# A gated cross-attention and feed-forward layer on one core: input loads, weight stores, a PSUM bank and the helpers of the first group rearranged

## The chip, the core and the metric

The kernel runs on one core of one Trainium2 chip. The metric is the device time in microseconds (us) of one execution. Before the change the median of three runs is 2418.64 us (2414.57 to 2418.65). The profile is that of one more execution on the same core.

The core has a matrix engine (TensorE, PE in the profile, with its weight loads shown as PEld), three engines for element-wise work (VectorE or DVE, ScalarE or ACT, GpSimd or POOL), and SyncE (SP), which in this kernel only starts DMAs. A DMA can be started from several engines; each engine starts its own in the order of its instructions, so a start that has to wait holds up the starts, and any work, behind it on the same engine. SBUF is the on-chip memory that the engines work from, PSUM the eight banks that TensorE writes its sums to. "Scratch" below is a DRAM area that the kernel writes first and reads later.

## What is computed

All numbers are fp32: B = 64 sequences, S = 128, DIM = 512, four heads of 128, INTER = 1408.

```python
def attention(x, k, v, Wh, wg_w, wo_w, gamma, beta):   # k = v = ctx
    Q, K, V = (einsum('bshd,hde->bshe', heads(t), Wh) for t in (x, k, v))
    scores = einsum('bshe,bthe->bhst', Q, K) / sqrt(hd)
    masked = scores * decay[None]
    A = maximum(abs(masked.sum(axis=0)), 1.0)          # summed over all 64 sequences
    O = einsum('hst,bthe->bshe', A, V).reshape(b, s, dim)
    Y = (O - mean) / sqrt(var + 1e-3) * gamma + beta
    return relu(x @ wg_w) * Y @ wo_w
def ffn(x):
    g, u = (x @ gate_w.T) * gate_s, (x @ up_w.T) * up_s
    return (silu(g) * u) @ down_w.T * down_s
x = x + tanh(g_xattn) * attention(layernorm(x), ctx, ctx, ...)
return x + tanh(g_ffn) * ffn(layernorm(x))
```

The sum over all sequences in `A` is why the kernel has two passes: no attention output can be formed before every score is in.

## The kernel before

**Groups.** The work goes by groups of four sequences (512 tokens), so there are 16 groups. Products of large matrices use Strassen and Winograd's scheme: a matrix is split in 2 x 2 blocks, sums of blocks are formed first, and seven products of half size take the place of eight. The sums of the weights are formed once in the first pass and kept (`wgc`, in SBUF) or written to scratch (`wo_scr`, `dn_scr`, `gu_scr`); the sums of the activations are formed for every group (`combine_a` L190, `combine_b` L184).

**First pass (L393 to L409).** For each group:
- `prepare` (L315): statistics of x by VectorE (L150), one rstd for the four sequences (VectorE L145, then a power on GpSimd L146), then for each sequence the normalised rows xn (VectorE L162), four transposes on TensorE (L157), and their copy to `xnT` (VectorE or ScalarE, L329 and L331).
- `scores` of the group before (L334): x by the Gram matrix of Wh (pq L338, copied by ScalarE to q), and then 16 matmuls (L348) that add context by q to `acc`. `acc` is the second half of the PSUM tile `banks_c` (L134, L313) and takes the sum over all groups.
- `project` of the group before (L358): relu(x @ wg) by seven products (L169) into bank_a, bank_f, bank_b and the *first* half of `banks_c`. VectorE adds m5 to two results (L379, L382), ScalarE copies or applies relu to the others, and two stores bring w to scratch `w_scr` (L388).

`interleave` mixes the steps of these three by given weights. The order on each engine is then decided by the scheduler of the framework, which also adds the waits: it knows a dependency by tile, so two instructions on different halves of `banks_c` can wait for each other.

**Loads and stores.** Loads of x (L96, five buffers), of the context (L102, five buffers), the weights, and all stores are started by SyncE, in one order; ScalarE starts only the constants of the beginning (L203 to L217, among them `wgc`). From group 2 on, one step of `prepare_weights` (L247) is taken at the end of each group's turn: first wo, then six steps of down weights, then five of gate/up weights. Each step loads raw blocks into one buffer (tag "prep", L256, L273, L296), has GpSimd form the sums (L290, L305), and starts the stores of these sums (L264, L289, L309) in the same step. The sums of `wgc` are formed at the very start (L230), on GpSimd too.

**Between the passes.** After the last scores, `attn` is made from `acc` (L412 to L415). Attention of group 0 and the projection of group 15 are interleaved (L534).

**Second pass.** `attention(g)` (L418) runs interleaved with `ffn(g-1)` (L570). Attention: pv (L428) and po (L438) per sequence, normalisation of po, transposes (L455), scale and shift by ScalarE (L460), the product with w by GpSimd (L465), the sums ys by GpSimd (L471), and seven products with wo into bx, bz and by (L478). m1, a copy of the first of them, is added to three quarters of x by GpSimd (L496) and the rest by VectorE (L489); then comes the second LayerNorm (L520 to L529), whose transposed result is `x1nT`. The sums of x1nT's blocks are GpSimd's (`combine_tokens`, L549). Ffn: five blocks j of seven products (L169), of which each begins with

```python
bank_c = next_c()                              # L593: the other half of banks_c
nc.scalar.copy(bank_c, bank_a)                 # L596
product(bank_f, w[GS1], t[:, 0], True)         # L597
```

then the hidden values (L583, L584) and their sums, the rest of gate and up (L631), seven products with the down weights (L648) and, at the very end of a group, two stores of 512 KB (L697).

Of the kernel before, what the change touches and what calls it, by code (L numbers as in the profile page):

```python
# [1 line left out]

# [25 lines left out]
def interleave(*weighted):  # L28

    runs = [[gen, steps, 0] for gen, steps in weighted if gen is not None]  # L30
    while runs:
        run = min(runs, key=lambda r: (r[2] + 1) / r[1])
        try:
            next(run[0])
            run[2] += 1
        except StopIteration:
            runs.remove(run)


@with_exitstack  # L40
def flamingo_gated_layer(
# [63 lines left out]
    x_next = load_x(0)  # L105
    c_next = [load_ctx(b) for b in range(GB)]
# [27 lines left out]
    banks_c = ps_bank.tile([P, 2, TOK], F32, name="banks_c")  # L134
    for seeded in (bank_b, banks_c[:, 0, :]):
        for i in range(TOK // P):
            nc.tensor.matmul(
                seeded[:, i * P : (i + 1) * P], lhsT=ident, rhs=ident,
                start=(i == 0), stop=True, skip_group_check=True,
            )  # L140
# [58 lines left out]
    wide1 = pass1.enter_context(tc.tile_pool(name="wide1", bufs=2))  # L199
# [5 lines left out]
    for m, k, e in ((GA11, 0, 0), (GA12, 1, 0), (7, 0, 1), (GA22, 1, 1)):  # L205
        for s in range(2):
            e0 = e * HN + s * P
            nc.scalar.dma_start(
                out=wgc[:, m, s],
                in_=wg[k * HN : (k + 1) * HN, e0 : e0 + P].rearrange("(k p) i -> p k i", p=P),  # L210
            )
    decay = once.tile([P, H, S], F32, name="decay")
    nc.scalar.dma_start(out=decay, in_=decayT)
# [3 lines left out]
    nc.scalar.dma_start(out=wh_sb, in_=wh.rearrange("h d e -> d h e"))  # L217
# [6 lines left out]
    for h in range(H):  # L224
# [5 lines left out]
    combine_a(  # L230
        nc.gpsimd, [wgc[:, m] for m in (GS1, GS2, GS3, GS4)],
        wgc[:, GA11], wgc[:, GA12], wgc[:, 7], wgc[:, GA22],
    )

    def constants():

        nc.sync.dma_start(out=gamma_sb, in_=gamma.rearrange("(c p) -> p c", p=P))
        nc.sync.dma_start(out=beta_sb, in_=beta.rearrange("(c p) -> p c", p=P))
        nc.sync.dma_start(out=gs_sb, in_=gate_s)
        nc.sync.dma_start(out=us_sb, in_=up_s)  # L240
        cols = slice(REST * P, INTER)
        for s, w in enumerate((gateT, upT)):
            nc.sync.dma_start(
                out=gu_rest[:, s], in_=w[:, cols].rearrange("(c p) i -> p c i", p=P)
            )

    def prepare_weights():  # L247

        constants()
        ds = once.tile([P, DIM], F32, name="ds")  # L250
        nc.sync.dma_start(out=ds, in_=down_s.partition_broadcast(P))
        nc.vector.tensor_scalar_mul(ds, ds, tanh_g[:, 1:2])
        yield


        raw = once.tile([P, NC, DIM], F32, tag="prep", name="wo_raw")  # L256
        nc.sync.dma_start(out=raw, in_=wo.rearrange("(c p) e -> p c e", p=P))
        nc.vector.tensor_scalar_mul(raw, raw, tanh_g[:, 0:1])
        t = once.tile([P, 4, KC, HN], F32, tag="prep2", name="wo_t")
        b = (  # L260
            raw[:, 0:KC, 0:HN], raw[:, 0:KC, HN:DIM], raw[:, KC:NC, 0:HN], raw[:, KC:NC, HN:DIM],
        )
        combine_b(nc.gpsimd, [t[:, i] for i in range(4)], *b)
        for m, src in ((DB11, b[0]), (DB21, b[2]), (DB22, b[3])):  # L264
            nc.sync.dma_start(out=wo_scr[m], in_=src)
        for i, m in enumerate((DT1, DT2, DT3, DT4)):
            nc.sync.dma_start(out=wo_scr[m], in_=t[:, i])
        yield


        for j in range(NJ + 1):
            i1, i2 = (j, NJ + j) if j < NJ else (REST, None)
            raw = once.tile([P, 2, DIM], F32, tag="prep", name="dn_raw")  # L273
            for q, i in enumerate((i1, i2)):
                if i is None:
                    nc.sync.dma_start(out=raw[:, q], in_=downT[i1 * P : (i1 + 1) * P])
                    nc.gpsimd.tensor_tensor(dn_rest, raw[:, q], ds, ALU.mult)
                    continue
                if j == NJ:
                    continue  # L280
                nc.sync.dma_start(out=raw[:, q], in_=downT[i * P : (i + 1) * P])
                nc.gpsimd.tensor_tensor(raw[:, q], raw[:, q], ds, ALU.mult)
            if j == NJ:
                yield
                continue
            t = once.tile([P, 4, HN], F32, tag="prep2", name="dn_t")
            b = (raw[:, 0, 0:HN], raw[:, 0, HN:DIM], raw[:, 1, 0:HN], raw[:, 1, HN:DIM])
            combine_b(nc.gpsimd, [t[:, i] for i in range(4)], *b)
            for m, src in ((DB11, b[0]), (DB21, b[2]), (DB22, b[3])):  # L289
                nc.sync.dma_start(out=dn_scr[m, :, j], in_=src)  # L290
            for i, m in enumerate((DT1, DT2, DT3, DT4)):
                nc.sync.dma_start(out=dn_scr[m, :, j], in_=t[:, i])
            yield

        for j in range(NJ):
            w = once.tile([P, 8, 2, KC, P], F32, tag="prep", name="gu_raw")  # L296
            i1 = slice(j * P, (j + 1) * P)
            i2 = slice((NJ + j) * P, (NJ + j + 1) * P)
            k1, k2 = slice(0, HN), slice(HN, DIM)
            for s, mat in enumerate((gateT, upT)):  # L300
                for m, k, i in ((GA11, k1, i1), (7, k1, i2), (GA22, k2, i2), (GA12, k2, i1)):
                    nc.sync.dma_start(
                        out=w[:, m, s], in_=mat[k, i].rearrange("(c p) i -> p c i", p=P)
                    )
            combine_a(  # L305
                nc.gpsimd, [w[:, m] for m in (GS1, GS2, GS3, GS4)],
                w[:, GA11], w[:, GA12], w[:, 7], w[:, GA22],
            )
            nc.sync.dma_start(out=gu_scr[0][j], in_=w[:, 0:3])  # L309
            nc.sync.dma_start(out=gu_scr[1][j], in_=w[:, 3:7])  # L310
            yield

    acc = banks_c[:, 1, :].rearrange("p (h s) -> p h s", h=H)  # L313

    def prepare(g, x_t, xnT):  # L315

        for j in range(GB):
            bn(mean_var[:, g * GB + j, :], x_t[j // 2][:, j % 2, :])
        cols = slice(g * GB, (g + 1) * GB)
        inv_std(rstd[:, cols], mean_var[:, cols, 1], LN_EPS, GB)  # L320
# [37 lines left out]
    def project(g, xnT):  # L358
# [6 lines left out]
        bank_c = banks_c[:, 0, :]  # L365
# [21 lines left out]
        for q in range(2):  # L387
            nc.sync.dma_start(out=w_scr[g, q], in_=w[:, q])  # L388
# [4 lines left out]
    for g in range(NG):  # L393
        x_t, c_t = x_next, c_next
        xnT = wide1.tile([P, NC, TOK], F32, tag="xT", name="xnT")
        prep = prepare(g, x_t, xnT)
        next(prep)
        after = (g + 1) % NG
        x_next = load_x(after)
# [5 lines left out]
        c_next = [load_ctx(after * GB + j) for j in range(GB)]  # L405
        pending = (g, c_t, xnT)
        if g >= 2:
            next(weights, None)
# [9 lines left out]
    def attention(g, x_t, c_t, x1nT):  # L418

        yT = att.tile([P, NC, TOK], F32, tag="yT", name="yT")  # L420
        for q in range(2):
# [28 lines left out]
            for d in range(2):  # L450
# [14 lines left out]
                nc.gpsimd.tensor_tensor(y, w[:, d], y, ALU.mult)  # L465
# [5 lines left out]
        combine_a(nc.gpsimd, [s[:, i] for i in range(4)], a11, a12, a21, a22)  # L471
# [24 lines left out]
        for q, d in ((0, d2), (1, d1), (1, d2)):  # L496
            add(nc.gpsimd, q, d, m1)
# [34 lines left out]
    x_t, c_t = x_next, c_next  # L532
    x1nT = wide.tile([P, NC, TOK], F32, tag="xT", name="x1nT")
    interleave(  # L534
        (attention(0, x_t, c_t, x1nT), ATT_STEPS), (project(pending[0], pending[2]), 7)
# [9 lines left out]
    def next_c():  # L545
        turn[0] ^= 1
        return banks_c[:, turn[0], :]

    def combine_tokens(x1nT):  # L549

        t = comb.tile([P, 4, KC, HT], F32, tag="t", name="tcomb")
        b = as_b(x1nT)
        combine_b(nc.gpsimd, [t[:, i] for i in range(4)], *b)
        return b[0], b[2], b[3], t
# [15 lines left out]
    def ffn(g, x_t, x1nT, tokens):  # L570
# [87 lines left out]
        def down_rest(bank, q, cols):  # L658
            for i in range(2):
# [4 lines left out]
                    start=False, stop=(i == 1), skip_group_check=True,  # L664
# [27 lines left out]
        yield from down_product(bank_c, DT4, h22, False)  # L692
        down_rest(bank_c, 1, d1)
        add(1, d1, bank_c)
        for q in range(2):
            b = g * GB + 2 * q
            nc.sync.dma_start(out=out[b : b + 2].rearrange("b s d -> s b d"), in_=x_t[q])  # L697
# [3 lines left out]
    pending = (0, x_t, x1nT, combine_tokens(x1nT))  # L701
    x_next = load_x(1)
    c_next = [load_ctx(GB + j) for j in range(GB)]
    for g in range(1, NG):
        x_t, c_t = x_next, c_next
        x1nT = wide.tile([P, NC, TOK], F32, tag="xT", name="x1nT")
        if g + 1 < NG:
            x_next = load_x(g + 1)
# [6 lines left out]
        pending = (g, x_t, x1nT, combine_tokens(x1nT))  # L715
# [59 lines left out]
```

## Time and profile before

| | |
|---|---|
| median of three runs | 2418.64 us (2414.57 to 2418.65) |
| the profiled execution | 2416.87 us |
| its span, first to last instruction | 2415.1 us |
| mean granted clock of TensorE | 0.994 |
| TensorE busy: matmuls, weight loads | 2351.8 us (97%), 1996.3 us (83%) |
| VectorE, ScalarE, GpSimd busy | 802.0, 587.2 and 686.2 us (33%, 24%, 28%) |
| moved by DMA | 396.31 MB, mean 164 GB/s |
| load of x, 512 KB: from start to landing | 5.0 us (median of 64) |
| load of context, 256 KB | 3.0 us (median of 128) |
| store of w, 512 KB | 3.7 us (median of 32) |
| chain of work that ended last | TensorE 85%, VectorE 5%, GpSimd 4%, DMA 3% |

The page cuts the span into 40 slices of 60.4 us. In the rows of slices a digit is the busy share of an engine in tenths, and 9 means 90% or more; in the row PEclk it is the clock that was granted to TensorE, in tenths of full speed. The first pass with the join takes about the first seven slices (to 420 us), the second pass the rest, at 125.38 us a group.

Rows of instructions are read like this: the time of the start, the duration, the engine with the line of the code, the operation, its output and inputs by the program's names, and in brackets how long the engine had been idle just before and what ended that. A row of waits names the waiting instruction, then what it waited for, and behind it the total in us, the number of times and the longest. In a table by windows each engine has its busy time and, in brackets, the number of instructions, in the order PE, PEld, DVE, ACT, POOL; behind them stand the mean clock, the DMA engines' busy share and the GB/s that they moved. "SPq" marks a DMA that SyncE starts.

### The profile page before, as it was taken

Reading aid. Unit: us, or ns where it says so; the run is one execution under the profiler, and the core shown is the slowest. Engines: PE = TensorE matmul, PEld = TensorE weight load, DVE = VectorE, ACT = ScalarE, POOL = GpSimd, SP = SyncE. Lnnn points to the kernel's source line nnn. Section 1 sums busy time; section 2 is a strip of 40 time slices with the busy share of each in tenths; the row PEclk is TensorE's granted clock in tenths of the full one; section 3 lists DMA queues with packets and bytes.
Section 4 is the critical chain, followed back from the end, with each engine's and each line's share of the span. In section 5 each row is a group of like instructions: output and inputs, shape, how many; then the busy total and the mean of one; then the engine's idle time right before and its main releaser. Section 6 shows DMA issues by size and latency. Waiting matters only on the chain.

```text
span 2415.1 us, 28827 instructions
## 1 busy us (share of the span) xinstructions
PE 2351.8 (97%) x11480; PEld 1996.3 (83%) x11480; DVE 802.0 (33%) x1541; ACT 587.2 (24%) x1076; POOL 686.2 (28%) x770
## 2 busy tenths in 40 slices
PE   7899998999999999999999999999999999999999
PEld 6777787888888888888888888888888888888887
DVE  6455433232323232323232323232323233232321
ACT  2232332312122222222221313131313131312121
POOL 3433003332323232323241414141414132232320
PEclk9999999999999999999999999999999999999999
DMA  7777544545454545444545444454545454544342
GB/s 262 243 251 251 172 144 131 214 131 185 139 173 150 176 143 173 146 166 148 168 157 165 164 146 162 159 168 140 175 145 165 140 178 133 182 133 149 118 147 72
DMA packets 136262, 396.31 MB, mean 164 GB/s; under 512 B 14272, under 2 KB 33856, under 8 KB 125248
## 3 DMA queue, kind: packets, MB, share of 16 engines
q1 hardware_dynamic: 132464, 392.63, 49.1%
q10 hardware_dynamic: 3664, 1.84, 0.3%
q8 instruction: 91, 1.49, 0.3%
q14 instruction: 43, 0.35, 0.0%
HBM read 345.26 MB, written 49.15 MB: 163 GB/s over the span
## 4 chain that ended last, share of the span: by engine, by line
PE 85%; DVE 5%; POOL 4%; DMA 3%; issue 1%; ACT 1%; SPq 0%; ACTq 0%; POOLq 0%; DVEq 0%
PE banks_c L169 17%; PE bank_a L169 12%; PE banks_c L648 9%; PE bank_b L169 6%; PE bank_a L648 6%; PE bank_f L169 4%; PE by L478 3%; PE bank_b L648 3%; PE bank_f L648 3%; PE pv L428 2%; PE bank_f L631 2%; PE bank_a L631 2%; PE bz L478 2%; PE bx L478 2%; PE banks_c L348 2%; PE po L438 2%
## 5 line engine op out<-in xcount | busy, mean ns | idle before, releaser
L169 PE MATMUL banks_c<-tcomb,gu 128*128 128x256 f32 x1920 | 453.9, 379 | 0.0
L169 PEld LDWEIGHTS banks_c<-tcomb,gu 128*128 128x128 f32 x1920 | 358.9, 190 | 46.3 <-ACT bank_b L604 0.7
L169 PE MATMUL bank_a<-x1nT,gu 128*128 128x256 f32 x1280 | 305.2, 381 | 6.8 <-ACT banks_c L596 6.7
L169 PEld LDWEIGHTS bank_a<-x1nT,gu 128*128 128x128 f32 x1280 | 237.6, 191 | 41.5 <-ACT banks_c L596 12.4
L146 POOL TENSOR_TENSOR rs<-ve,mhalf 128x1 f32<-128x1 f32 x128 | 72.5, 575 | 608.0 <-DVE ve L145 606.1
L191 POOL TENSOR_TENSOR hs<-h,h 128x256 f32<-128x256 f32 x80 | 58.0, 725 | 517.0 <-DVE h L584 517.0
L583 ACT ACTIVATE sil<-c,gs_sb 128x256 f32<-128x256 f32 x160 | 81.3, 508 | 345.1 <-DVE c L613 237.2
L169 PE MATMUL bank_b<-x1nT,gu 128*128 128x256 f32 x640 | 151.2, 379 | 0.0
L169 PE MATMUL bank_f<-tcomb,gu 128*128 128x256 f32 x640 | 151.2, 379 | 0.0
L613 DVE TENSOR_TENSOR c<-banks_c,m 128x512 f32<-128x512 f32 x80 | 55.3, 691 | 279.7 <-PE banks_c L169 279.7
L648 PE MATMUL banks_c<-dn_w,hs 128*128 128x256 f32 x640 | 146.0, 379 | 0.0
L648 PE MATMUL bank_a<-dn_w,h 128*128 128x256 f32 x640 | 143.5, 379 | 0.0
L648 PEld LDWEIGHTS bank_a<-dn_w,h 128*128 128x128 f32 x640 | 120.3, 190 | 16.3 <-issue 0.7
L169 PEld LDWEIGHTS bank_f<-tcomb,gu 128*128 128x128 f32 x640 | 120.5, 190 | 15.8
L169 PEld LDWEIGHTS bank_b<-x1nT,gu 128*128 128x128 f32 x640 | 120.5, 190 | 15.8
L648 PEld LDWEIGHTS banks_c<-dn_w,hs 128*128 128x128 f32 x640 | 119.2, 190 | 15.2 <-ACT bank_b L682 0.3
L596 ACT COPY banks_c<-bank_a 128x512 f32<-128x512 f32 x80 | 45.6, 570 | 301.6 <-PE bank_a L169 242.9
L584 DVE SCALAR_TENSOR_TENSOR h<-c,us_sb,sil 128x256 f32<-128x256 f32 x160 | 89.5, 559 | 83.8 <-ACT sil L583 83.8
L465 POOL TENSOR_TENSOR yT<-w_t,yT 128x512 f32<-128x512 f32 x64 | 81.1, 1268 | 121.3 <-ACT yT L460 121.3
L150 DVE BATCH_NORM_STATS2 st<-x_t 128x6 f32<-128x512 f32 x128 | 82.4, 683 | 82.2 <-DMA x_t<-in_x_dram 81.1
L584 DVE SCALAR_TENSOR_TENSOR h<-bank_a,us_sb,sil 128x256 f32<-128x256 f32 x80 | 38.6, 482 | 209.1 <-ACT sil L583 209.1
L188 POOL TENSOR_TENSOR tcomb<-x1nT 128x512 f32<-128x512 f32 x32 | 39.9, 1267 | 205.6 <-ACT x1nT L528 205.6
(134 smaller groups left out, 3651.9 us busy)
## 6 DMA issues: line engine op xcount, KB each, us to landing
gu<-gu_scr SPq DMA_DIRECT2D x80, 1024.0 KB, 4.9
dn_w<-dn_scr SPq DMA_DIRECT2D x112, 640.0 KB, 3.9
gu<-gu_scr SPq DMA_DIRECT2D x80, 768.0 KB, 4.3
x_t<-in_x_dram SPq DMA_DIRECT2D x64, 512.0 KB, 5.0
c_t<-in_ctxT_dram SPq DMA_DIRECT2D x128, 256.0 KB, 3.0
wo_w<-wo_scr SPq DMA_DIRECT2D x112, 256.0 KB, 2.8
w_scr<-w SPq DMA_DIRECT2D x32, 512.0 KB, 3.7
w_t<-w_scr SPq DMA_DIRECT2D x32, 512.0 KB, 3.6
```

The costliest lines, as they stand in the source:

```text
L146: nc.gpsimd.tensor_tensor(dst, ve, mhalf[:, :n], ALU.pow)
L150: nc.vector.bn_stats(st, src)
L169: nc.tensor.matmul(bank[:, s * HT : (s + 1) * HT], lhsT=w[:, s, k, :], rhs=rhs[:, k, :], start=(start and s == 0 and k == 0), stop=(s == 1 ...
L191: engine.tensor_tensor(s[0], a21, a22, ALU.add)
L348: nc.tensor.matmul(acc[:, h, :], lhsT=c_t[j][:, h, :], rhs=qs[h][:, j * S : (j + 1) * S], start=(g == 0 and j == 0 and h == 0), stop=(g == ...
L465: nc.gpsimd.tensor_tensor(y, w[:, d], y, ALU.mult)
L478: nc.tensor.matmul(bank[:, i * HN : (i + 1) * HN], lhsT=lhs[:, k, i * P : (i + 1) * P], rhs=w[:, k, :], start=(start and i == 0 and k == 0 ...
L583: nc.scalar.activation(sil, src[:, 0:n], AF.Silu, scale=gs_sb[:, i : i + 1])
L584: nc.vector.scalar_tensor_tensor(dst, src[:, n : 2 * n], us_sb[:, i : i + 1], sil, ALU.mult, ALU.mult)
L613: nc.vector.tensor_add(c22, bank_c, m5)
L631: nc.tensor.matmul(bank, lhsT=gu_rest[:, s, c, :], rhs=x1nT[:, c, :], start=(c == 0), stop=(c == NC - 1),)
L648: nc.tensor.matmul(bank[:, i * HN : (i + 1) * HN], lhsT=lhs[:, j, i * P : (i + 1) * P], rhs=dn[:, j, :], start=(start and i == 0 and j == ...
```

## The change

- **Loads.** Two groups of x are loaded at the start, and in the first pass x of group g+2 is loaded behind the work of group g (before: group g+1, ahead of that work). The x pool keeps its five buffers. `wgc` is loaded through SyncE, behind the first two groups of x, and the first context behind it. The constants (down_s, decay, wh and the others) are loaded in group 1.
- **Stores of w** are started by ScalarE.
- **Weights.** `prepare_weights` becomes a list of parts: wo, then down and gate/up by turns for j = 0 to 4, then the rest of down. In each step the stores of the part *before* are started, the sums of this part are formed and the next part is loaded. The raw blocks have two buffers, the sums one. The step is taken ahead of the group's work. The sums of `wgc` are formed in group 1.
- **The score bank.** `banks_c` becomes the two tiles `bank_c0` and `bank_c1`; `acc` is `bank_c1`. In the second pass the two are used by turns as the halves were.
- **rstd of group 0** is computed in two halves.
- **First group.** In attention of group 0, VectorE forms ys and, for d = 1, the product with w; it also makes the first `combine_tokens`. m1 is added to the quarters in another order, in all groups. The projection of group 15 begins seven steps later in the interleaving.
- **The end.** In every group the first half of the output is stored before the last down product. In the last group the second half is stored in three pieces: the columns d2 before the last product, then 128 KB after each half of it; the rest of the down product is taken first.

```diff
-    x_next = load_x(0)
-    c_next = [load_ctx(b) for b in range(GB)]
+    x_next = [load_x(0), load_x(1)]
...
-    banks_c = ps_bank.tile([P, 2, TOK], F32, name="banks_c")
-    for seeded in (bank_b, banks_c[:, 0, :]):
+    bank_c0 = ps_bank.tile([P, TOK], F32, name="bank_c0")
+    bank_c1 = ps_bank.tile([P, TOK], F32, name="bank_c1")
+    for seeded in (bank_b, bank_c0):
...
-            nc.scalar.dma_start(
+            nc.sync.dma_start(
                 out=wgc[:, m, s],
...
+    def prepare_weights():
+        parts = [(load_wo, sum_wo)]
         for j in range(NJ):
+            parts.append((partial(load_down, j), partial(sum_down, j)))
+            parts.append((partial(load_gu, j), partial(sum_gu, j)))
+        parts.append((load_down_rest, sum_down_rest))
+        raw, stores = parts[0][0](), []
+        yield
+        for n, (_, sums) in enumerate(parts):
+            for dst, src in stores:
+                nc.sync.dma_start(out=dst, in_=src)
+            stores = sums(raw)
+            if n + 1 < len(parts):
+                raw = parts[n + 1][0]()
+            yield
...
+        n = GB if g else 2
         for j in range(GB):
             bn(mean_var[:, g * GB + j, :], x_t[j // 2][:, j % 2, :])
-        inv_std(rstd[:, cols], mean_var[:, cols, 1], LN_EPS, GB)
+            if (j + 1) % n == 0:
+                cols = slice(g * GB + j + 1 - n, g * GB + j + 1)
+                inv_std(rstd[:, cols], mean_var[:, cols, 1], LN_EPS, n)
...
-            nc.sync.dma_start(out=w_scr[g, q], in_=w[:, q])
+            nc.scalar.dma_start(out=w_scr[g, q], in_=w[:, q])
...
         next(prep)
-        after = (g + 1) % NG
-        x_next = load_x(after)
+        if g == 1:
+            gate_weights()
+            constants()
+        elif g > 1:
+            next(weights, None)
         interleave(
...
+        x_next.append(load_x((g + 2) % NG))
+        c_next = [load_ctx((g + 1) % NG * GB + j) for j in range(GB)]
         pending = (g, c_t, xnT)
-        if g >= 2:
-            next(weights, None)
...
+        helper = nc.vector if g == 0 else nc.gpsimd
...
-                nc.gpsimd.tensor_tensor(y, w[:, d], y, ALU.mult)
+                (helper if d else nc.gpsimd).tensor_tensor(y, w[:, d], y, ALU.mult)
...
-        combine_a(nc.gpsimd, [s[:, i] for i in range(4)], a11, a12, a21, a22)
+        combine_a(helper, [s[:, i] for i in range(4)], a11, a12, a21, a22)
...
-        for q, d in ((0, d2), (1, d1), (1, d2)):
+        for q, d in ((1, d2), (0, d2), (1, d1)):
             add(nc.gpsimd, q, d, m1)
...
-        (attention(0, x_t, c_t, x1nT), ATT_STEPS), (project(pending[0], pending[2]), 7)
+        (attention(0, x_t, c_t, x1nT), ATT_STEPS),
+        (after(7, project(pending[0], pending[2])), 14),
...
-        return banks_c[:, turn[0], :]
+        return (bank_c0, bank_c1)[turn[0]]
...
+        nc.sync.dma_start(out=out[b : b + 2].rearrange("b s d -> s b d"), in_=x_t[0])
...
+        nc.sync.dma_start(
+            out=out[b + 2 : b + 4, :, d2].rearrange("b s d -> s b d"), in_=x_t[1][:, :, d2]
+        )
+        down_rest(bank_c, 1, d1, stop=False)
+        dn = down(DT4)
+        for i in range(2):
...
+            dst = x_t[1][:, i, d1]
+            nc.vector.tensor_add(dst, dst, half)
+            nc.sync.dma_start(out=out[b + 2 + i, :, d1], in_=dst)
```

## The prediction

> **What bounds the kernel now.** I read the page's forty slices first, then the waits by engine for the first 500 us and for the rest, then the busy times by window. Last came the timeline around the largest gap of each kind.
>
> ```profile
> PE   7899998999999999999999999999999999999999
> ...
> PEclk9999999999999999999999999999999999999999
> ```
>
> TensorE (PE) is busy 2351.8 of 2415.1 us. The change takes no matmul away, so at most 63.3 us of idle time, plus what a low granted clock costs, is to be had. The waits say where it lies. First the first 500 us (waited for: us, times, longest), then the same for 500 to 2415 us:
>
> ```profile
> PE banks_c L348 <- DVE w L379: 19.3, 10, 4.7
> PE pt L157 <- DVE xn L162: 11.8, 3, 9.7
> PE pg L225 <- DMA whT_sb<-in_whT_dram: 5.7, 1, 5.7
> PE bz L478 <- POOL ys L191: 2.9, 1, 2.9
> PE bz L478 <- DVE x_t L489: 1.8, 1, 1.8
> ```
> ```profile
> PE pt L455 <- DVE xn L162: 6.3, 14, 0.5
> PE bank_a L169 <- ACT banks_c L596: 6.2, 14, 0.4
> ```
>
> So there are four places: the start, the first pass, the join of the passes, and 0.9 us per group of the second. The first pass's wait is seen in VectorE's timeline (start, length, idle before it) and SyncE's:
>
> ```profile
> 82.63 0.38 SPq L96 DMA_DIRECT2D x_t<-in_x_dram  x1
> ...
> 88.01 0.69 DVE L150 BATCH_NORM_STATS2 st<-x_t 128x6 f32<-128x512 f32 x1 [6.41 <-DMA x_t<-in_x_dram]
> 88.62 0.67 DVE L379 TENSOR_TENSOR w<-banks_c,m5p 128x512 f32<-128x512 f32 x1
> ...
> 89.35 1.34 PE L348 MATMUL banks_c<-q,c_t 128*128 128x128 f32 x8 [3.87 <-DVE w L379]
> ```
>
> VectorE stood at the statistics of an x tile whose load was issued late; L379 queued behind. TensorE waited for L379 although L348 writes the *other* bank of `banks_c`: one tile, one dependency.
>
> **A. Start: 6.5 us less.** Now GpSimd's first rstd (18.25) waits behind four gate sums, whose operands land at 14.4; transposes start at 20.85, bank_a at 24.11. After, rstd comes in halves ahead of the sums. Statistics at 5.1 to 9.4 (rows as now), half an rstd about 0.7 (0.58 for one column, 1.03 for four), the second group's statistics and four xn of 0.55: transposes from about 12.4, bank_a from about 16.1, 8.0 earlier. Against it: group 1's rstd is now behind the sums. Wgc moves to SyncE's queue behind 2 MB of x and lands at about 14 again; sums 4 x 1.26 end at 19.2, rstd 1.1, xn 0.55, transposes at 21 where TensorE is ready at 19.3: 1.5 us given back. Bounds 4 to 8.5.
>
> **B. First pass: 13 us less.** TensorE is idle 20.0 us between 40 and 300 (260 less 240.04 busy), and runs at 0.91 and 0.94 of its clock from 80 to 120 (about 2.5 us): 22.5 us are there. An undisturbed group costs 20.8 us: seven products of 1.73, eight pq of 0.43, sixteen acc matmuls (3.5), sixteen transposes (1.75).
>
> The split tile removes the false wait; VectorE may then be late until the next bank_a product needs xnT. "Two groups ahead" buys less than it says. There are still five x buffers, and the built order shows the statistics moved ahead as well: those of a group stand three groups early, three or four VectorE instructions after the xn that frees the buffer. By the rows above that xn ends 8.4 us into a group and bank_a's last xnT copy is due at 19.05; statistics, L382 and the copy take 3.1. So a landing 7.6 us after the release costs nothing; x takes 5.0 now.
>
> What is late next is the weight preparation. A gate/up part is a chain on one buffer, now:
>
> ```profile
> 205.97 1.45 SPq L302 DMA_DIRECT2D gu_raw<-in_gateT_dram  x3
> ...
> 229.39 1.45 SPq L302 DMA_DIRECT2D gu_raw<-in_gateT_dram  x3
> ```
>
> That is 23.4 us a turn: issue 4.5, landing 3.9, sums 6.1 (the last store is issued at 220.48), store 8.0, and the rest. After, the two raw buffers alternate between down and gate/up parts, so gate/up keeps one and keeps this chain; only its store is less crowded (5.3 to 6.5 estimated from 1 MB at 335 GB/s and c_t's 3.0 for 256 KB): 20 to 21.5 us. But a down part now rides in each turn: 1.4 + 2.8 MB of weights and 3 MB of x, c and w, 7.2 MB. The best 20 us stretch moved 320 GB/s (DMA share 0.89): 22.5 us. I take 23 us. In SyncE's order the x load stands behind the gate/up stores, so five turns set the step: 5 x (23 - 20.8) = 11, less a slack of 1.5: 9.5 us stay. 22.5 - 9.5 = 13. Bounds: turn 21 us, gain 20; turn 25 us, 3.
>
> Also here: the stores of w go to ScalarE, about 1 us of issue per group (SyncE takes 1.4 to 2.3 for two) on an engine with 7.3 of 20 us busy. Each names one of eight DMA semaphores and so waits for a DMA eight earlier; queued behind is the copy of bank_a, due 3 us or more later. Zero while SyncE keeps pace; beyond 3 us every us is TensorE's. The weight stores a step later no longer hold x loads (14.6 us of SyncE waiting for GpSimd at L290 between 74 and 120); that is in the turn.
>
> **C. Join: 7 us less.** Idle from 395 to 430 is 2.86 + 1.82 + 1.90 + 2.2 (pv and po waiting for ACT's v) + 0.25 = 9.0 us, and:
>
> ```profile
> 420.00:425.00 5.00, 4.27 (x23) 3.78 (x24) 0.44 (x1) 1.76 (x3) 3.08 (x3) 0.63 0.43 132
> 425.00:430.00 5.00, 4.27 (x20) 3.98 (x20) 1.84 (x4) 0.59 (x1) 2.41 (x3) 0.50 0.99 412
> ```
>
> (TensorE's clock is the third number from the end.) On VectorE the y product and the first sum take 0.68 each instead of 1.27: bz has its operand at 399.3 instead of 402.2. GpSimd then adds m1 at once, so the 1.82 goes too. The Trainium skill (SBUF — State Buffer, "Who interferes with whom") speaks against this: a VectorE instruction with two SBUF inputs and a GpSimd instruction that reads SBUF exclude each other for a whole instruction. The trace agrees in kind: sums L188 on VectorE average 1.00 and 0.80 us in the first pass, 0.66 alone. By the uncontended row the operand comes at 399.3; by the rule, behind a y product and an m1 add of 1.27 each, at 400.6; three of the four projection matmuls left for here (1.3 us) cover the difference. The four matmuls, bx and five more products (1.7 + 1.7 + 8.7) run from 399.4 to 411.5; x's last statistics, rstd, xn and transposes take 5 us (416.35 to 421.2 now). First gate/up weights follow the last w store: last product 409.7, relu, 3.7 us landing: loads issued about 414.6 instead of 423.2, block there at 419.5. bank_a starts at about 420 instead of 430.3; but pv and po worth 2.4 us, done now before it, come later: 7.9, less about 1 for the clock, still low. Combining tokens on VectorE (2.7 instead of 5 us) is inside. Bounds 3 to 11.
>
> **D. Second pass: 6.7 us less.** Each of 15 groups shows this:
>
> ```profile
> 601.25 0.55 PE L455 MATMUL pt<-ident,xn 128*128 128x128 f32 x3 [0.45 <-DVE xn L162]
> 601.62 0.57 ACT L596 COPY banks_c<-bank_a 128x512 f32<-128x512 f32 x1 [2.09 <-DVE h L584]
> ...
> 602.25 1.99 PE L169 MATMUL bank_a<-x1nT,gu 128*128 128x256 f32 x8 [0.45 <-ACT banks_c L596]
> ```
>
> The copy waits for L584, which reads the other bank: the same false dependency. In the new order the copy stands four ScalarE instructions earlier and bank_a waits for nothing: 15 x 0.45 = 6.7. xn's chain is unchanged, so its 0.45 stays; bounds 0 (the slip absorbs it) and 13.5. Order of the m1 adds: nothing waits there now, zero.
>
> **E. End: 1.5 us less.** The last matmul ends at 2410.41, the 512-column add takes 0.69, the 512 KB store ends 3.97 us later. After, the last piece is a 256-column add (0.4) and 128 KB. The skill (DMA: Bandwidth & Descriptors, "Bandwidth") says to batch to 1 MiB and (in "Anatomy of one DMA") gives about 2.0 us fixed; pieces cost more in total. Only the last counts: dn_scr's 128 KB stores land in 2.7 to 3.6 here, so 1.0 on the store and 0.3 on the add; by the skill's formula 3.2 against 2.3: 0.9 and 0.3. I take 1.5 because the queue is empty. Bounds 0.5 to 2.2.
>
> **Sum.** 6.5 + 13 + 7 + 6.7 + 1.5 = 34.7. The profiled execution took 2416.87 us (span 2415.1 and 1.8 around): 2382.2. The median of the runs, 2418.64, lies 1.8 above it, so 2384.
>
> **Rivals.**
> 1. *The turn hides* (0.22). DMA keeps up, first pass gains 20; perhaps xn's wait slips too. 2416.9 - 41.7 + 1.8 = 2377, with xn 2370. For it: 395 GB/s in single 2 us stretches. Against: 7.2 MB in 20.8 us is 346 GB/s sustained.
> 2. *The wait changes its name* (0.2): five buffers feed the loads no earlier, VectorE stands at the statistics, TensorE waits for xnT instead of L379. First pass gains 3: 2394. For it: VectorE waits 71.3 us for x in 20 waits. Against: half is slack now.
> 3. *SyncE's queue loses* (0.04), the slower case. Down stores, down loads and gate/up stores stand in one in-order queue with x; down sums before gate/up sums, or rstd (waiting for x behind the stores), would make a turn 30 us or more. The other parts and the 22.5 give 44.2 us; five turns use them up at 20.8 + 8.8 = 29.6 us. At 32: 2418.6 - 44.2 + 56 = 2430. Against: the built order puts gate/up sums first.
> 4. *Nothing measurable* (0.02): turns at about 29.5.
>
> **Numbers.** The main case has 0.52 and by itself 2376 to 2391. The range 2368 to 2400 takes rivals 1 and 2 in. 0.2% (4.8 us) is about what a measurement of this kernel can tell from no change: faster 0.94, same 0.02, slower 0.04.
>
> **What would show it.** A right: transposes near 12.4, bank_a near 16. B: no row "banks_c L348 <- DVE w L379"; idle TensorE only in about five groups, together near 10 us, DMA over 300 GB/s there, later groups at 20.8. C: bz unwaited, first gate/up bank_a about 10 us closer to the last score. D: the ACT copy's wait gone, xn's 0.45 in place. E: under 3 us from last add to end. It is wrong if the five turns take over 25 us, if new waits for xnT or ScalarE's queue reach 15 us, or if the join still runs at half clock for 10 us.

## The result, and the profile after

The changed kernel takes 2377.77 us (median of 4 runs, 2374.89 to 2380.06), the kernel before 2416.61 us (median of 4). The ratio is 0.9841 with a 95% interval of 0.9821 to 0.9860. The forecast was 2384 in a range of 2368 to 2400.

The profiled execution took 2374.89 us (span 2373.1, mean granted clock 0.998), 42.0 us less span than before; the prediction's sum was 34.7. Its slices of TensorE and of its clock:

```profile
PE   8999999999999999999999999999999999999999
...
PEclk9999999999999999999999999999999999999999
```

The start is fuller, and the two slices of 8 further on, in the first pass and at the join, are gone. The largest waits of TensorE in the first 500 us (waited for: us, times, longest), and then all from 500 us on:

```profile
PE pt L165 <- DVE xn L170: 6.8, 3, 3.3
PE pq L374 <- DVE xnT L365: 6.1, 3, 4.0
PE pg L230 <- DMA whT_sb<-in_whT_dram: 5.7, 1, 5.7
PE bank_c L177 <- DVE w L415: 3.3, 1, 3.3
PE bz L520 <- DVE ys L199: 1.4, 1, 1.4
```
```profile
PE pt L497 <- DVE xn L170: 6.3, 14, 0.5
PE bank_c L753 <- DVE x_t L758: 0.5, 1, 0.5
```

The row of scores waiting for L379 (19.3 us) has no successor. New are 9.4 us in four waits for xnT (L365) and w (L415), at 87, 112, 157 and 182 us. In the second pass the copy's row is gone, xn's stays. Cut at the same events, the two profiles stand so:

| stretch | before | after | gained | predicted |
|---|---|---|---|---|
| A: to the end of group 0's last pq | 33.1 | 27.5 | 5.6 | 6.5 |
| B: on to the end of the last score | 343.7 | 328.4 | 15.3 | 13 |
| C: on to group 0's bank_b addition (L669, now L713) | 170.7 | 161.7 | 9.0, of which 0.7 is D's | 7 |
| D: on to the same addition of group 15 | 1857.7 | 1846.5 | 11.2, and C's 0.7 | 6.7 |
| E: on to the end | 9.8 | 9.1 | 0.7 | 1.5 |

One thing has to be known before profiles are compared. In all profiles here but one, TensorE is granted half its clock now and then in A, B or C, for about 3.4 us or a multiple of it, and its work then takes twice as long: at 111.91 us in the changed kernel four matmuls pq take 3.75 us, else 1.88. The cost is half the time that TensorE is busy in such stretches. In B it is 3.4 us before and 2.9 in the changed kernel, in C 4.4 and nothing; D has none. Where these stretches fall differs from profile to profile.

### The profile page after: what moved, and what is told of

The parts are those of the page before. It is cut to its first block, busy times and chain, and to the rows that moved or that the text cites. A ratio compares the mean times of both kernels' runs of the same rounds, so it can differ in the third digit from the quotient of the medians.

```text
span 2373.1 us, 28824 instructions
## 1 busy us (share of the span) xinstructions
PE 2336.3 (98%) x11480; PEld 1992.0 (84%) x11480; DVE 800.8 (34%) x1553; ACT 588.6 (25%) x1076; POOL 674.0 (28%) x761
## 4 chain that ended last, share of the span: by engine, by line
PE 90%; DVE 4%; POOL 3%; DMA 2%; issue 1%; ACT 0%; SPq 0%; POOLq 0%; DVEq 0%
PE bank_c L177 18%; PE bank_a L177 13%; PE bank_c L692 9%; PE bank_b L177 7%; PE bank_a L692 6%; PE bank_f L177 5%; PE by L520 3%; PE bank_b L692 3%; PE bank_f L692 3%; PE pq L374 2%; PE bz L520 2%; PE pv L470 2%; PE bank_f L675 2%; PE bank_a L675 2%; PE bx L520 2%; PE pt L165 2%
## 5 line engine op out<-in xcount | busy, mean ns | idle before, releaser
L177 PE MATMUL bank_c<-tcomb,gu 128*128 128x256 f32 x1920 | 453.8, 379 | 0.0
L177 PEld LDWEIGHTS bank_c<-tcomb,gu 128*128 128x128 f32 x1920 | 358.9, 190 | 46.3 <-ACT bank_b L648 0.6
L657 DVE TENSOR_TENSOR c<-bank_c,m 128x512 f32<-128x512 f32 x80 | 55.3, 691 | 273.0 <-PE bank_c L177 273.0
L692 PE MATMUL bank_c<-dn_w,hs 128*128 128x256 f32 x640 | 146.0, 379 | 0.0
L692 PEld LDWEIGHTS bank_c<-dn_w,hs 128*128 128x128 f32 x640 | 119.2, 190 | 15.2 <-ACT bank_b L726 0.3
L640 ACT COPY bank_c<-bank_a 128x512 f32<-128x512 f32 x80 | 45.6, 570 | 318.6 <-PE bank_a L177 318.6
L177 PE MATMUL bank_c<-t,wgc 128*128 128x256 f32 x384 | 92.7, 383 | 3.3 <-DVE w L415 3.3
```

The costliest lines, as they stand in the source:

```text
L177: nc.tensor.matmul(bank[:, s * HT : (s + 1) * HT], lhsT=w[:, s, k, :], rhs=rhs[:, k, :], start=(start and s == 0 and k == 0), stop=(s == 1 ...
L657: nc.vector.tensor_add(c22, bank_c, m5)
L692: nc.tensor.matmul(bank[:, i * HN : (i + 1) * HN], lhsT=lhs[:, j, i * P : (i + 1) * P], rhs=dn[:, j, :], start=(start and i == 0 and j == ...
```

## The experiments

All times are medians of 4 or 5 runs, with the kernel before beside them on the same chip. B, C and the group period are from one profile each, cut as above. How far B can be trusted is seen in three kernels whose first pass is the same: changed, join as before and one last store have 328.4, 327.0 and 331.2.

| kernel | us | ratio to before (95%) | B | C | period in D |
|---|---|---|---|---|---|
| before | 2416.61 | 1 | 343.7 | 170.7 | 125.38 |
| changed | 2377.77 | 0.9841 (0.9821 to 0.9860) | 328.4 | 161.7 | 124.67 |
| bank split alone | 2398.16 | 0.9926 (0.9914 to 0.9939) | 342.2 | 169.1 | 124.71 |
| bank joined again | 2400.33 | 0.9935 (0.9923 to 0.9948) | 339.2 | 162.5 | 125.38 |
| old weight order | 2396.91 | 0.9921 (0.9907 to 0.9935) | 350.2 | 163.0 | 124.67 |
| weights paced | 2365.01 | 0.9791 (0.9777 to 0.9804) | 316.3 | 164.5 | 124.68 |
| two parts per group | 2380.49 | 0.9845 (0.9832 to 0.9859) | 331.2 | 163.2 | 124.71 |
| w stored by SyncE | 2365.34 | 0.9786 (0.9773 to 0.9800) | 314.0 | 165.9 | 124.67 |
| two parts, w by SyncE | 2366.73 | 0.9797 (0.9784 to 0.9810) | 314.0 | 165.9 | 124.67 |
| own gate/up buffers | 2373.53 | 0.9826 (0.9810 to 0.9841) | 327.0 | 162.9 | 124.67 |
| join as before | 2379.70 | 0.9844 (0.9831 to 0.9858) | 327.0 | 165.9 | 124.67 |
| paced, start and end | 2362.12 | 0.9770 (0.9756 to 0.9783) | 316.2 | 161.6 | 124.68 |
| and later transposes | 2351.91 | 0.9734 (0.9719 to 0.9748) | 317.0 | 162.3 | 124.00 |
| one last store | 2375.72 | 0.9836 (0.9819 to 0.9852) | 331.2 | 161.6 | 124.67 |

**The bank split alone**, on the kernel before:

```diff
-    banks_c = ps_bank.tile([P, 2, TOK], F32, name="banks_c")
+    bank_c0 = ps_bank.tile([P, TOK], F32, name="bank_c0")
+    bank_c1 = ps_bank.tile([P, TOK], F32, name="bank_c1")
```

> The kernel before, with only the score bank split in two tiles. Theory (the tile was one dependency in both passes, and a wait of 0.45 us costs TensorE 0.71 us): the second pass gains 15 x 0.71 = 10.6 us, its group period goes from 125.38 to 124.67 us. In the first pass the rows for banks_c waiting for L379 are gone; part of that wait comes back as a wait for xnT or xn, because the x loads are as late as they were: 3 to 10 us gained of 22. Sum about 17 us: 2400 us. Rival (the wait only changes its name in the first pass): 10.6 us and nothing else, 2406 us, with 15 us or more of waits for xnT before 300 us.

Measured 2398.16, 17.0 us below the kernel before on that chip: the theory's sum. The period is 124.71, so the second pass gained what the theory says. In the first pass the profile seems to speak for the rival: B gained 1.5 us, and 17.6 us of waits for w and xnT stand where 19.3 for w stood. But it is the profile of the slowest of the five runs (2401.16 us). Stretch B in a table by windows, the kernel before and then this one:

```profile
33.10:376.80 343.70, 323.47 (x1695) 261.65 (x1694) 166.18 (x304) 108.69 (x178) 79.00 (x69) 0.99 0.66 218
```
```profile
30.60:372.80 342.20, 323.66 (x1695) 265.64 (x1694) 168.30 (x304) 108.81 (x178) 78.97 (x69) 0.97 0.65 219
```

The clock is lower: half of it for 20.5 us, against 6.8 before, which costs 8.2 us instead of 3.4. With the clock of before, B would have gained about 6 us. The idle time fell by just 1.7 of these (waits did change their names); the rest are stalls that no row shows, taken up under B below.

**The bank joined again**, the reverse edit on the changed kernel:

> The changed kernel with the score bank joined in one tile again. Theory: the second pass loses 10.6 us, and the first pass loses what the split brought there on top of the loads and the weights, 3 to 8 us: about 2394 us (changed kernel 2377.8). Rival (earlier loads had taken the wait away by themselves, the split matters only in the second pass): 2388 us, and no row in the first pass in which the scores wait for L379's counterpart. Other rival (the split is what the whole first pass gained): 2403 us.

Measured 2400.33, between the theory and the other rival. The period is 125.38 again, and B is 10.9 us longer at the same clock, with 15.5 us of scores waiting for w. In the first pass the split is thus worth about 6 us alone and about 11 with the rest of the change. As B differs by 4 us between profiles of one and the same first pass, this does not show that the parts fail to add.

**The weight preparation of before** on the changed kernel: the parts in their old order (wo, all of down, all of gate/up), one raw buffer, the stores in the step of the sums, the step at the end of a group.

> The changed kernel with the weight preparation of before: one raw buffer, stores in the step of the sums, all down parts and then all gate/up parts, step at the end of a group. Theory (the stores a step later and two raw buffers keep SyncE's queue from holding x loads while GpSimd forms sums): the first pass loses 4 to 10 us, about 2385 us, spread over eleven groups and not over five. Rival (the split bank and the loads two groups ahead did it; the order of the weights is indifferent): 2376 to 2379 us. Second rival (the new order crowds ten parts in five groups, the old one spreads them, so undoing it helps): 2370 us.

Measured 2396.91, 19 us more and beyond my bounds; the first pass is longer than before the change (350.2). Of the 21.8 us that B is longer than in the changed kernel, 6.0 are half clock. VectorE stands 104.8 us at x between 20 and 300 us, up to 13.7 at once. With the old order of the weights, the split bank and the loads two groups ahead together bring nothing in B.

**The weights paced**: each step is held behind the last x load of the group before.

```diff
         elif g > 1:
-            next(weights, None)
+            with tc.issue_after(last_x[0].ins):
+                next(weights, None)
```

> The changed kernel with each step of the weights queued behind the last x load of the group before, so that one part and not two are moved in a group. Theory (what TensorE still waits for between 80 and 160 us, 9.1 us and a lower clock beside it, comes from five turns of 7 MB in 24 us, in which x lands up to 9 us after its issue): 8 to 11 us less than the changed kernel, about 2368 us, groups at 20.9 us. Rival (the five x buffers make VectorE stand at the statistics whatever the weights do): no change, 2377 us, with the same waits for xnT.

Measured 2365.01: the groups run at 20.9 us from the second on, except one of 22.3. This fits the theory, but it does not show that bytes were the cause. For that I kept the order and doubled the parts:

```diff
             with tc.issue_after(last_x[0].ins):
                 next(weights, None)
+                next(weights, None)
```

> The paced kernel (2365.0 us), but with two parts of the weights in each step, still queued behind the last x load of the group before. It moves as much in a group as the changed kernel does, in the order of the paced one. Theory (bytes in a group count: 7 MB do not fit in 20.9 us): 2374 to 2379 us, waits of 7 us or more between 60 and 200 us. Rival (the order of x loads in SyncE's queue was all that the pacing mended): 2365 to 2368 us.

Measured 2380.49, as the theory has it, but by another way: TensorE waited 9.8 us for ScalarE's q. ScalarE stood about 7 us in two groups in front of a store of w. One of these rows (start, length, idle before and what ended it):

```profile
139.06 0.60 ACT L424 ACTIVATE w<-bank_c 128x512 f32<-128x512 f32 x1 [6.83 <-DMA gu_raw<-in_upT_dram]
```

The store is issued at 138.69, ahead of this relu on ScalarE's queue, and by the profile it had waited for a weight load to land. That is the risk of step B that I had priced at zero. So the stores of w had to be looked at by themselves.

**The stores of w on SyncE again**, on the changed kernel:

```diff
-            nc.scalar.dma_start(out=w_scr[g, q], in_=w[:, q])
+            nc.sync.dma_start(out=w_scr[g, q], in_=w[:, q])
```

> The changed kernel with the stores of w started by SyncE again. Theory (1 us of starts per group, on a queue that holds up x loads only in the five crowded groups): 0 to 4 us more, 2378 to 2382 us. Rival (the stores wait for relu results of ScalarE, and while they stand in SyncE's order, x loads and weights behind them wait too, in every group): 5 to 15 us more, 2383 to 2393 us. A gain would show that ScalarE's queue paid for them.

Measured 2365.34: a gain of 12 us where I expected a loss. TensorE has no wait at all between 23 and 365 us. Busy time by window (PE, PEld, DVE, ACT, POOL; then clock, DMA share, GB/s), first the changed kernel, then this one:

```profile
100.00:120.00 20.00, 15.96 (x68) 11.69 (x67) 9.45 (x15) 5.29 (x9) 12.19 (x11) 0.83 0.95 320
```
```profile
100.00:120.00 20.00, 20.00 (x106) 16.46 (x105) 10.58 (x21) 7.29 (x12) 6.85 (x7) 1.00 0.92 319
```

The DMA engines are as full, and between 60 and 160 us they move 31.72 MB against 31.46. TensorE is busy without a break. It is not the bytes. The same edit on the kernel with two parts per group:

> The kernel with two parts of the weights in each group (2380.5 us), with the stores of w started by SyncE and not by ScalarE. There TensorE waited 9.8 us for ScalarE's q, and ScalarE stood up to 7 us at a store of w that waited for a weight load. Theory (two parts and two x loads in each turn of SyncE's order bind a group to the turn, whoever starts the stores): 2374 to 2381 us, the waits for q turn into waits for xnT or w. Rival (the stores on ScalarE's queue were the cost, as they may be in the changed kernel): 2363 to 2368 us, groups at 20.9 us.

Measured 2366.73, the rival's value; 31.33 MB in the same 100 us, and no wait. My theory of the turn has fallen: two parts and 24 to 26 us between the pairs of x loads cost nothing here.

**Two buffers of their own for gate/up**, on the changed kernel (wo shares them, down has one):

> The changed kernel with two buffers of its own for the raw gate/up blocks (wo shares them, down has one of its own); SyncE's order is unchanged. Theory A (a turn is the chain on one buffer: loads, sums, stores, and SyncE waits 14.2 us in all for these stores before it can issue the next loads): the turn falls from 24 us to 21 or 22 us, 6 to 10 us less, about 2370 us. Theory B (7.2 MB at 300 to 330 GB/s take 22 to 24 us whatever the buffers): the turn stays at 23.5 to 24 us, 2376 to 2379 us.

The gate/up stores follow each other in 23.3 us instead of 23.8, and the time is 2373.53; its interval overlaps the changed kernel's. That is near theory B: the one buffer sets little of the turn.

**The join as before**:

```diff
-        helper = nc.vector if g == 0 else nc.gpsimd
+        helper = nc.gpsimd
...
-        (after(7, project(pending[0], pending[2])), 14),
+        (project(pending[0], pending[2]), 7)
```

> The changed kernel with the join of the passes as before: GpSimd forms ys, the products with w and the first sums of tokens, m1 is added to group 0 in the old order, and group 15's projection is not delayed. Theory (the stretch from the last score to the end of group 0's feed-forward, 170.7 us before and 161.7 after, gained 8.3 us beside the split bank): 8 us more, 2386 us. Rival (VectorE and GpSimd hold each other up when both read SBUF, so moving the sums gains little, and most of the 8.3 us came from less crowded loads): 2 us more, 2380 us.

Measured 2379.70, the rival's value, which can't be told from the changed kernel. In the profile C is 4.2 us longer, but two stretches at half clock, of which the changed kernel's C has none, make 3.3 of that; TensorE's idle time in C is 7.6 us against 6.1. So the join's own edits are worth one or two us; whether they also keep the clock up is not shown (see C below).

**Start and end mended**, on the paced kernel: on GpSimd only the first sum of wgc stands ahead of group 1's rstd, and the second half of the last product goes to bank_f, to which ScalarE copies what has been summed so far.

```diff
+        nc.gpsimd.tensor_tensor(s1, a21, a22, ALU.add)
+        with tc.issue_after(last_rs[0].ins):
...
+        nc.scalar.copy(bank_f[:, 0:HN], bank_c[:, HN:TOK])
```

> The paced kernel (2365.0 us) with two edits: of the sums of wgc only the first stands ahead of group 1's rstd on GpSimd, and the second half of the last down product has its own bank, so that it need not wait for the addition that reads the first half. Theory (TensorE's wait for group 1's xn, 3.3 us, is GpSimd's 5.7 us of sums, less what VectorE needs; the wait at the end is one bank, one dependency): 1.5 to 3 us less at the start, 0.7 us less at the end, about 2362 us. Rival (VectorE is as late there as GpSimd, and the addition's write is what the product waits for): 2365 us.

Measured 2362.12, 2.9 us less. In the profile the start gained 4.4 us: xn's wait is 1.65 us instead of 3.27, and between 20 and 25 us the clock is 1.00 where it was 0.62. The clock makes 2.9 of the 4.4. The end gained nothing: a wait of 0.45 us for the copy took the place of the 0.51.

**The transposes later**, on that kernel: those of the second pair of sequences stand two products further on in TensorE's order.

```diff
+                with tc.issue_after(last_mm[0].ins):
                     for c in range(KC):
```

> The kernel with paced weights and mended start and end (2362.1 us), in which the transposes of attention's second pair of sequences stand behind two more feed-forward products in TensorE's order. Theory (a wait of 0.45 us of which TensorE's pipeline makes 0.71 us, in 15 groups): the last regular wait of the second pass is gone, 10.6 us less, period 123.97 instead of 124.67 us, about 2351.5 us. Rival (what hangs on these transposes, the product with w, ys and bz, is then late, and the wait only moves there): within 3 us of 2362, with new rows for bz or bx. Second rival (only the shown 0.45 counts): 2355.4 us, period 124.2.

Measured 2351.91, 10.2 us less by the medians and 8.3 by the profiled spans, and the period is 124.00. This is the fastest version, 25.9 us below the changed kernel. From 400 us on one row of waits is left:

```profile
PE bank_c L767 <- ACT bank_f L762: 0.4, 1, 0.4
```

**One last store** of 256 KB instead of two of 128:

> The changed kernel with the last two 128 KB stores and their two additions as one of each (512 columns, 256 KB). Theory (the pieces save 1.5 us behind the last matmul, but 0.5 us of wait and about 0.2 us of refilling are given back, since the second half's matmuls wait for the addition on the first half of the same bank): 0 to 1 us more, which the medians can't tell; in the profile the stretch from the last rest product to the end is 10.2 us now and 10.5 to 11 then. Rival (the store's size doesn't matter at this end): the stretch is shorter, 9.5 to 10 us.

From the last bank_b product to the end it takes 10.1 us, as the changed kernel (10.15) does. Neither expectation holds: the pieces bring nothing, and lose nothing.

## Why the prediction was right, and where it was not

**A, 6.5 predicted, 5.6 measured.** Transposes began at 11.8 (12.4 predicted) and bank_a at 14.7 (16.1). Group 1 gave back more than the 1.5 us of the sum: the four sums ended at 20.0 (19.2 predicted), rstd took 1.4 (1.1), so TensorE waited 3.3 us. In this profile half clock came on top, 1.7 us. Ten of the kernels have this start, and TensorE waits 3.27 to 3.49 us at this place in all of them; seven profiles then show half clock and three don't. First the paced kernel, after a wait of 3.27 us, then the one with w stored by SyncE, after 3.29 us:

```profile
20.00:25.00 5.00, 2.72 (x9) 2.39 (x10) 4.09 (x9) 0.59 (x1) 1.45 (x2) 0.62 0.87 222
```
```profile
20.00:25.00 5.00, 2.75 (x13) 2.15 (x14) 4.09 (x9) 1.17 (x2) 1.41 (x2) 1.00 0.89 243
```

The Trainium skill (TensorE: Matmul & The Clock Gate, "Part 1: The HAM clock gate") has the clock halve after an idle window of about 3.4 us, and says that this window runs freely. Waits of just under its length that sometimes cost clock and sometimes don't agree with that; the wait of 1.65 us cost none in either kernel that has it. With this start A ends between 25.9 and 28.8 us, so its gain is 4.4 to 7.2, and 6.5 is within it.

**B, 13 predicted, 15.3 measured; the cause of the remainder was wrong.** I had 22.5 us in the stretch and 9.5 staying. The best run of it here takes 314.0 us, without idle time or half clock, so 29.7 were there, and 14.4 stayed. First the changed kernel (the kernel before is shown above), then the one with w stored by SyncE:

```profile
27.50:355.80 328.30, 318.88 (x1700) 262.89 (x1699) 152.39 (x294) 108.97 (x178) 76.48 (x69) 0.99 0.68 229
```
```profile
25.90:339.90 314.00, 314.00 (x1696) 260.92 (x1696) 163.65 (x300) 109.47 (x178) 80.01 (x69) 1.00 0.72 239
```

Of the 29.7, TensorE was idle for 20.2, half clock cost 3.4, and 6.1 were stalls that no row shows; of the 14.4 the same three are 9.4, 2.9 and 2.0. Two things were missed.

The first is in the 22.5: those stalls. Late groups before took 21.4 to 21.5 us without a wait, and take 20.9 with the split bank, alone or with the rest. In the second pass it can be seen. Kernel before, last group (start, length):

```profile
2333.99 1.89 PE L169 MATMUL bank_f<-tcomb,gu 128*128 128x256 f32 x8
...
2335.90 1.99 PE L169 MATMUL bank_a<-x1nT,gu 128*128 128x256 f32 x8
2337.73 0.59 PE L169 MATMUL banks_c<-tcomb,gu 128*128 128x256 f32 x2
```

Eight matmuls follow each other in 1.73 us. Here ScalarE's copy into banks_c ends at 2335.85, held up by L584 on the other half, and the product behind it starts 1.91 us behind the one before it, and the next 1.83 behind that: 0.28 us lost, with no bracket of idle time, since the drawn end of a product overlaps the start of the next by 0.16 us.

The second is the step "Zero while SyncE keeps pace". It failed: I took the lower of its two ends, and in the crowded groups the stores of w on ScalarE's queue cost 12 to 14 us, as both runs that moved them back show (12.4 and 13.8 by the medians), at the same number of bytes. With the weights spread thin (paced) they cost 2.3 us at most. In the changed kernel the loss is seen at VectorE, in the place that rival 2 named. An x load starts at 99.87; then (start, length, idle before) VectorE and TensorE:

```profile
108.87 1.28 DVE L158 BATCH_NORM_STATS2 st<-x_t 128x6 f32<-128x512 f32 x2 [7.61 <-DMA x_t<-in_x_dram]
...
111.09 0.68 DVE L365 COPY xnT<-pt 128x512 f32<-128x512 f32 x1
...
111.91 2.04 PE L374 MATMUL pq<-xnT,gram 128*128 128x512 f32 x2 [4.04 <-DVE xnT L365]
```

x lands 9 us after its start, statistics stand ahead of the copy, and the scores wait for the copy. In the runs with w on SyncE, x lands in 5.6 to 6.0 us instead of 7.4 (medians of 60 to 160 us), and VectorE waits at most 6.0 us for it. Which of three things does it in the changed kernel, the slower landing, SyncE's order or VectorE's order, stays open: moving the stores changes all three, and no run parted them. ScalarE too is seen to stand in the changed kernel, though not at the start of a store:

```profile
96.40 0.60 ACT L409 ACTIVATE w<-bank_a 128x512 f32<-128x512 f32 x1 [3.24 <-DMA dn_scr<-dn_t]
```

This relu writes into the one buffer of w, and the store of w that started at 88.11 had landed at 96.29, so that store is the likelier end of the wait than the one named. TensorE has no gap beside it; only with two parts per group does it wait for ScalarE's q. Rival 1 was right that the turn can hide, and wrong about the way: no 346 GB/s are needed.

**C, 7 predicted, 8.3 measured; about half the size is the clock.** Stretch C by windows: before, changed, paced (the same join as changed), and changed with the join as before:

```profile
376.80:547.50 170.70, 161.39 (x788) 136.62 (x787) 56.29 (x115) 43.91 (x80) 60.56 (x66) 0.97 0.48 159
```
```profile
355.80:517.50 161.70, 155.60 (x784) 132.26 (x783) 66.00 (x126) 43.68 (x80) 49.24 (x56) 1.00 0.50 168
```
```profile
345.00:509.60 164.60, 158.50 (x785) 134.58 (x784) 66.05 (x126) 43.67 (x80) 49.27 (x56) 0.98 0.48 165
```
```profile
354.60:520.50 165.90, 158.32 (x785) 134.75 (x784) 56.34 (x116) 43.68 (x80) 60.63 (x66) 0.98 0.49 164
```

Idle time fell from 9.3 to 6.1 us. Another 4.4 us are the half clock of before from 421 us on, which the changed kernel's profile lacks; I had written "still low" and taken 1 us off for it. That it is lacking is in part luck: with the same join the paced kernel lost 3.1 us to the clock, and the kernels with this join and w on ScalarE's queue have C from 161.6 to 164.5. The join's own edits are seen in the idle time, 1.5 us against the join as before. With w on SyncE again C is 4.2 us longer: 1.7 of clock, 1.2 of idle time, and 0.9 because four matmuls of the last projection fall behind the cut. Gate/up loads then stand behind the last stores of w: they start 45.6 us after the last score, 37.5 in the changed kernel and 46.4 before. But TensorE waits just 0.2 us for them, so what this is worth stays open. On ys I took the row, and the rule was nearer. GpSimd, VectorE and TensorE of the changed kernel:

```profile
378.54 4.74 POOL L531 TENSOR_TENSOR x_t<-x_t,m 128x512 f32<-128x512 f32 x3 [1.06 <-ACT m L537]
...
378.84 1.63 DVE L199 TENSOR_TENSOR ys<-yT 128x512 f32<-128x512 f32 x1
...
380.62 1.97 PE L520 MATMUL bz<-wo_w,ys 128*128 128x256 f32 x8 [1.41 <-DVE ys L199]
```

The sum takes 1.63 us instead of 0.69 while GpSimd adds m1, and GpSimd 1.58 for each instead of 1.27: both are slowed. ys is there 5.2 us after the first wo product began; the row had given 3.2, the rule 4.5. The 1.4 us that I had covered by projection matmuls were not covered.

**D, 6.7 predicted, 11.9 measured.** The mechanism was right, the term mis-sized. A wait that the profile shows with 0.45 us costs 0.71: 0.16 more because the drawn end overlaps the next start, and 0.10 because the first product after it takes 1.83 us and not 1.73. Fifteen of these are 10.6, and four blocks of the last group with the unshown 0.28 are 1.1, together 11.7. The later transposes confirm it: another row of 0.45 us removed, another 0.69 per group.

**E, 1.5 predicted, 0.7 measured.** Additions and landing went as priced (last addition to end 3.1 us instead of 4.7; the formula that I used from the skill, which its page fits to DMAs started by GpSimd, gave 3.2 and 2.3 for stores that landed in 4.0 and 2.7), but the change made a new wait. Both halves of the last product are in one bank:

```profile
2367.51 2.43 PE L753 MATMUL bank_c<-dn_w,h 128*128 128x256 f32 x10 [0.51 <-DVE x_t L758]
```

The second half waits for the addition that reads the first. Again two halves of one tile wait for each other, but here they share one bank, and no run shows whether the wait could be left out within it. With its 0.51 us and the refilling, half of the pieces' gain is gone.

**The sum** came out 7 us low: D's term by 5.2, B by 2.3 from two errors that partly cancel, C by 1.3, A and E 1.7 the other way. That the total was so near is in part luck: D and the removal of the false waits in B were understood, but what stayed in B had another cause than the one I gave, and C reached its size through the clock. Rival 3, the slower case, did not come: nothing stood 30 us.

## What to carry to other kernels

A tile that holds two things is one dependency for both; look for waits whose releaser wrote the other half, and price each by what the next fixed event moves, not by the idle time that is shown. A DMA start on a computing engine's queue is free only while the DMA that its wait names has landed: in crowded stretches try it on the other queue before the bytes are blamed. Removing one wait on an in-order engine can uncover the next under another name, so judge a part by the time of the whole and not by the row that is gone. And before two profiles are compared, take out the clock: it makes up to 8.9 us in B and 5.8 in C between the kernels here, and the run that was profiled can be the slowest of its five.

## What the runs showed of the hardware

The 128x512 sum of two SBUF operands on VectorE took 0.69 us alone and 1.63 beside GpSimd's additions, which took 1.58 each instead of 1.27. Half clock came in stretches of about 3.4 us or a multiple; after waits of 3.27 to 3.49 us at one place it came in seven profiles of ten. TensorE moved without a break at 313 to 317 GB/s of DMA traffic for 100 us, with the DMA engines 0.9 busy or more: the traffic by itself did not slow it. The stores at the end landed 2.7, 3.2 and 4.0 us after the last addition for 128, 256 and 512 KB; but in the run with w on SyncE the one of 128 KB took 3.1, so a difference of 0.5 us is no more than one profile can be off.
